# Four graph layers on one core: a first batch of its own, and 64-row products issued in blocks

## The chip, the core and the metric

The kernel runs on one core of one Trainium2 chip. The metric is device time in microseconds of that core, the median of several executions. Engines are named as in the profile: PE (TensorE; PEld its weight loads), DVE (VectorE), ACT (ScalarE), POOL (GpSimd), and SP (SyncE), which issues most DMAs.

## What is computed

There are 16 independent graphs ("batches") of N = 1024 nodes with D = 128 features, and a dense 1024 x 1024 matrix `adj` each, of which about 1.6% is nonzero. Four layers follow each other; each normalises `x`, applies relu, and adds its result to `x`. Cut to what matters:

```python
h = relu(layernorm(x))                       # before every layer
# layer 0: columns of adj, degree from its rows
x += relu(concat(h, (adj.T @ h) / adj.sum(-1)) @ W0.T + b0)
# layer 1: rows of adj
x += leaky(((adj / adj.sum(-1)) @ h) @ W1.T + b1)
# layer 2: two rounds l of edge scores; only nonzero adj[n, m] matter
s[n, m] = sigmoid(relu(a[n] + b[m] + be1[l]) @ We2[l] + be2[l])   # a, b: h @ We1[l]
msg = (adj * s) @ h ;  h = layernorm(h + mlp([h, msg]))
x += h
# layer 3: attention over the nonzeros, softmax by rows, elu
x += elu(softmax(masked(leaky((Wh1 + Wh2.T) * (adj + I)))) @ Wh)
```

## The kernel before

N is cut into T = 8 tiles of P = 128 nodes. Layer 2 is the large one. It handles the 36 unordered tile pairs (28 off the diagonal, 8 on it, `BUCKETS`) in nine groups of four (`GROUPS`), and keeps only nonzero edges, packed in slots (320 for a pair off the diagonal, 480 on it).

`first(b)` (line 1014) does layers 0 and 1 of a batch. It loads each row tile `at` and each column tile `ct` of `adj` (line 977), sums the rows and copies them (`deg`, line 1037), transposes them on PE (`tn`, 1040 and 1041), writes the transposed matrix to DRAM (`adjT`, 1043), marks the nonzero places (`has`, 1048) and multiplies column tiles by the features (`nb`, 545). `count` (1071) ranks the nonzeros, layer 1 reads `adjT` back as `l`, and `build` (1158) makes four 0/1 matrices per pair: `st` from `far` (1112, 1116), `onT` (1191), `omT` (1199) and `om` (1206), on PE, ACT and DVE in turn.

`main` and `round` run the two rounds of layer 2. `gather` (1334) makes the hidden values of a pair's edges: four products into one PSUM bank `pre` (1345 and 1351), then two `hid` operations on ACT and DVE (1366, 1367). `dots` (1375) turns them into scores with 24 or more one-column products. `scores` (1417) spreads them (`val`, 1443), and `scatter` (1451) places them back with products into the bank `p` (1488). For the second direction of a pair off the diagonal these products write only 64 of 128 partitions: six per pair, 24 per group. Seven of the nine groups have them, so there are 224 such sets in 16 batches and two rounds. `upd` (1495) and `messages` (1501) follow. `last(s, b)` (1573) is the end of layer 2 and layer 3 of a batch (`strip`, `e`, `hp`).

The order on each engine is not that of the program. `run` (1599) weaves the generators of batch b's `main`, batch b-1's `last` and batch b+1's `first`. Then the class `Issue` (66 to 297) takes all instructions of this part, gives each a cost (`costs`, 130), and walks through them with a ready list per engine (`walk`, 196), forward and backward for four passes; the plan with the earliest end becomes a fixed order of issue on every engine. A change between full and 64-row products costs 94 or 119 ns in that walk (`switched`, 192). Nothing is reordered at run time.

In `run`, batch 0 has a part of its own ahead of the loop: `first(0)` runs alone up to the start of its builds, with the small preparations in `scaled` (893) beside it. Its builds are then woven into batch 0's `main`.

A second program for inputs that do not fit the packed form (class `Pairs`) is built too, and does not run here.

Of the kernel before, what the change touches and what calls it, by code (L numbers as in the profile page):

```python
# [3 lines left out]

# [53 lines left out]

SIGNAL_NS = 45.0
RESULT_NS = {"PE": 163.0, "Activation": 120.0, "DVE": 88.0, "Pool": 80.0}  # L60
NARROW_NS, WIDE_NS, HELD_NS = 94.0, 119.0, 130.0
DMA_NS, DMA_NS_PER_BYTE, DMA_NS_BEHIND, DMAS = 1900.0, 3.9e-3, 3.3e-3, 8
PASSES = 4


class Issue:
# [3 lines left out]
    def __init__(self, tc, ops, fixed):  # L70
        self.tc, self.ops, self.fixed = tc, ops, fixed
        self.tiles = {t.name: t for t in tc.tiles}
        self.queue = [str(i.engine).split(".")[-1] for i in ops]
        self.kind = [type(i).__name__.removeprefix("Inst") for i in ops]
        self.links()
        self.costs()

    def span(self, arg):

# [50 lines left out]
    def costs(self):  # L130


        self.busy, self.late, self.form, self.bytes = [], [], [], []
        for op, queue, kind in zip(self.ops, self.queue, self.kind):
            out, form = op.outs[0].bass_ap, False
            n, late, size = self.size(op.outs[0]), RESULT_NS.get(queue, 0.0), 0
            aps = [a.bass_ap for a in op.ins if hasattr(a, "bass_ap")]
            psum = bool(aps) and aps[0].space == bass.MemoryType.PSUM
            if kind == "Matmult":
                n = self.size(op.ins[0])  # L140
                form = out.shape[0] < 128
                if op.ins[0].dtype == F32:
                    busy = max(n / 1.2 + 6, 112) * (1 if op.is_transpose else 2)
                else:
                    busy = 29 if form else max(n / 2.4 + 2.5, 25)
            elif kind == "DMACopy":
                size = n * WIDTH[op.outs[0].dtype] * out.shape[0]
                inside = all(a.space == bass.MemoryType.SB for a in (out, aps[0]))
                busy = 630 if inside else 470
                late = DMA_NS + size * DMA_NS_PER_BYTE - busy  # L150
            elif queue == "Activation":
                busy = n / 1.2 + (50 if psum else 92) + 92 * (len(aps) - 1)
            elif queue == "DVE":
                wide = [a for a in aps if a.size() > 128]
                fast = kind == "TensorScalarPtr" and len(wide) == 1 and not psum
                if kind in ("BNStats", "TensorReduce"):
                    n = self.size(op.ins[0])
                busy = n * (0.53 if fast else 1.0625) + 55 + 64 * (len(aps) - len(wide))
                rows = {v[1] for v in map(self.span, (*op.ins[:1], *op.outs[:1])) if v}
                busy += HELD_NS * (len(rows) > 1)  # L160
            else:
                busy = 1560
            self.bytes.append(size)
            self.busy.append(busy)
            self.late.append(busy + late)
            self.form.append(form)

    def joined(self):

# [20 lines left out]
        return users, turn, homes  # L190

    def switched(self, j, was, back):
        one, two = (self.form[j], was) if back else (was, self.form[j])
        return 0.0 if one == two else NARROW_NS if two else WIDE_NS

    def walk(self, rank, seq, back=False):

# [8 lines left out]
        free, sent, was = dict.fromkeys(queues, 0.0), [(0.0, 0.0, 0)] * DMAS, False  # L206

        def offer(j):

# [20 lines left out]
        for _ in range(n):  # L230
            at, q = min(
                (free[q] if now[q] else max(free[q], soon[q][0][0]), q)
                for q in queues if now[q] or soon[q]
            )
            while soon[q] and soon[q][0][0] <= at:
                heappush(now[q], heappop(soon[q])[1:])
            j = heappop(now[q])[1]
            more = 0.0
            if self.kind[j] == "DMACopy" and not back:
                at = max(at, sent[0][1])  # L240
                more = DMA_NS_BEHIND * sum(
                    n * (end - at) / (end - then) for then, end, n in sent if end > at
                )
                sent = sent[1:] + [(at, at + self.late[j] + more, self.bytes[j])]
            elif q == "PE":
                at += self.switched(j, was, back)
                was = self.form[j]
            start[j], free[q] = at, at + self.busy[j]
            line[q].append(j)
            end = at + (self.busy[j] if back else self.late[j] + more + SIGNAL_NS)  # L250
            freed = {}
            for name in self.uses[j]:
                users[name] -= 1
                over[name] = max(over.get(name, 0.0), end)
                if name not in turn:
                    continue
                tag = self.tiles[name].tag
                if name not in live:
                    live[name] = heappop(homes[tag])
                    freed.setdefault(tag, []).append(given[tag] + 1)  # L260
                    given[tag] += 1
                if not users[name]:
                    heappush(homes[tag], over[name])
                    freed.setdefault(tag, []).append(given[tag])
            for tag, keys in freed.items():
                for key in dict.fromkeys(keys):
                    for k in parked.pop((tag, key), ()):
                        offer(k)
            for k, lag in edges[j]:
                ready[k] = max(ready[k], at + lag + more * (lag > 0.0))  # L270
                waits[k] -= 1
                if not waits[k]:
                    offer(k)
# [27 lines left out]
def tile_four_gnn_layers(  # L301
# [22 lines left out]
    nc = tc.nc  # L324
    B, N, D = x.shape
    P = 128
# [117 lines left out]
    class Layers:  # L444
# [20 lines left out]
            return tile.rearrange("p (t d) -> p t d", d=P + 1)  # L465

        def small(self, shape, tag, name):
            return self.work.tile(shape, F32, tag=f"{tag}{self.lane}", name=name)

        def one(self, name):  # L470

# [327 lines left out]
    class Edges:  # L799
# [115 lines left out]
        def scale_terms(self):  # L915
# [15 lines left out]
            for l in range(L):  # L931
                for h in range(2):
# [4 lines left out]
            bnd = work.tile([P, L], F32, tag="end", name="bnd")  # L937
# [48 lines left out]
        def strip(self, name):  # L986

            if self.rows_of.get("c"):
                return flat(self.row("c", name))
            return self.work.tile([P, 2 * 3 * P], F32, tag="strip", name=name, bufs=1)  # L990

        def alone(self, lane, others):

# [20 lines left out]
        def first(self, b):  # L1014
# [2 lines left out]
            xt = self.work.tile([P, T, D], F32, tag="x", name=f"x_{b}")  # L1017
            nc.sync.dma_start(xt, x[b].rearrange("(t p) d -> p t d", p=P))
            for _ in lane.layer0_own(xt, name):
                if b:  # L1020
                    yield 1.3
            z, own = lane.z, lane.o
            yield 0

# [43 lines left out]
            s.x = self.kept(xt, "x", f"xk_{b}")  # L1068
            yield from self.build(s, has, name)

        def count(self, s, has, name):


# [11 lines left out]
            end = self.work.tile([P, nb], F32, tag="end", name=f"end_{name}")  # L1085
# [204 lines left out]
        class Group:  # L1290
# [43 lines left out]
            def gather(self, i):  # L1334
# [5 lines left out]
                for d in range(self.nd):  # L1340
                    pre = path.m.one(f"pre_{self.name}_{i}_{d}")

                    parts, _ = path.parts[u // Q]
                    for k in range(2):
                        nc.tensor.matmul(  # L1345
                            pre[:, :c], parts[:, k, u % Q, 1 - d], om,
                            start=(k == 0), stop=True, skip_group_check=True,
                        )
                    _, both = path.parts[t // Q]
                    for k, (at, first) in enumerate(((0, 0), (c - n, back))):  # L1350
                        ins = nc.tensor.matmul(  # L1351
                            pre[:, at : at + n], both[:, k, t % Q, d], st[:, first : first + n],
                            start=False, stop=True, skip_group_check=True,
                        )
                    if not self.diag:
                        hid = path.work.tile(
# [184 lines left out]

        def main(self, s, b):

            xT = self.back(self.m.scratch(f"xT_{b}"), s.xT)
            self.parts = [None] * NH
            for h, half in enumerate(self.halves_of(xT)):
                yield from self.split(self.m, 0, h, half, f"{b}")
# [269 lines left out]
```

## Time and profile before

| what | value |
|---|---|
| time, median of 3 runs | 4661.11 us (4647.63 to 4667.04) |
| the profiled execution | 4639.45 us, its span 4637.7 us, granted clock 0.982 |
| PE, DVE, ACT busy | 94%, 84%, 65% of the span |
| DMA | 603.41 MB, mean 130 GB/s |
| first `pre` of batch 0 | 124.6 us after the start of the span |
| from there to the first `pre` of batch 1 | 250.9 us |
| from a batch's first `pre` to the next one's, batches 1 to 14 | 278.8 to 285.0 us |
| from batch 15's first `pre` (4321.1 us) to the end | 316.6 us |

A busy share is a mean over stages with different limits, so the stages are looked at one by one below. In the profile a row such as `L1488 PE MATMUL p<-omT,val 128*64 128x128 fp8e4` names line, engine, operation, what is written and read, the columns of the array that are used (64 of 128) and the moving operand. Matmuls overlap, so their mean durations are longer than the time from the start of one to the start of the next.

### The profile page before, as it was taken

What the parts mean: (1) busy time and instruction counts of PE and PEld (TensorE: products, weight loads), DVE (VectorE), ACT (ScalarE), POOL (GpSimd) and SP (SyncE); (2) the same over time, 40 slices, a digit from 0 to 9 for tenths busy, and PEclk for the clock granted to TensorE, in tenths of its full rate; (3) what the DMA queues carried; (4) which work ended last, traced back from release to release, by engine and by line L of the source; (5) the groups of instructions that cost most, each with busy time, mean ns of one, the idle gap of its engine ahead of it and who ended that gap; (6) DMA issues with size and microseconds to landing.
All of it is one profiled execution on the core that took longest, in us unless ns stands there. A gap on an engine that the chain in (4) does not pass through costs nothing.

```text
span 4637.7 us, 132212 instructions
## 1 busy us (share of the span) xinstructions
PE 4359.0 (94%) x53685; PEld 3581.9 (77%) x53685; DVE 3873.0 (84%) x9128; ACT 2992.3 (65%) x7238; POOL 194.4 (4%) x137
## 2 busy tenths in 40 slices
PE   6999999999999999999999999999999999999986
PEld 5787778777787777878878787777877777788765
DVE  4777797987979889797897979879797897979977
ACT  5666575675756767576675766757576675766643
POOL 0000100000000000000000000000000000000000
PEclk7999999999999999999999999999999999999997
DMA  7262635445363542635436353453634436344221
GB/s 213 66 198 68 196 94 164 114 127 162 90 185 100 147 142 83 196 107 147 126 94 198 89 162 115 130 165 85 189 103 140 142 83 196 107 145 123 80 80 57
DMA packets 852857, 603.41 MB, mean 130 GB/s; under 512 B 128528, under 2 KB 782608, under 8 KB 852240
## 3 DMA queue, kind: packets, MB, share of 16 engines
q1 hardware_dynamic: 847136, 593.24, 44.3%
q8 instruction: 423, 6.93, 0.6%
q10 hardware_dynamic: 5104, 1.65, 0.1%
q14 instruction: 194, 1.59, 0.1%
HBM read 446.44 MB, written 100.66 MB: 118 GB/s over the span
## 4 chain that ended last, share of the span: by engine, by line
PE 63%; DVE 21%; ACT 6%; DMA 6%; issue 2%; SPq 1%; POOL 1%; ACTq 0%; DVEq 0%; POOLq 0%
PE pre L1345 8%; PE nb L545 8%; PE p L1488 7%; PE msg L441 7%; PE sc L1391 5%; PE pre L1351 5%; DVE hid L1367 4%; PE h L599 4%; DVE val L1443 3%; PE hp L441 3%; PE bb L553 2%; PE xn L608 2%; PE tn L1040 2%; DMA at<-in_adj_dram 2%; DMA both<-part 2%
## 5 line engine op out<-in xcount | busy, mean ns | idle before, releaser
L1367 DVE SCALAR_TENSOR_TENSOR hid<-pre,hid 128x320 f16<-128x320 f32 (+1 forms) x2048 | 1004.1, 508 | 168.6 <-ACT hid L1366 157.9
L1366 ACT ACTIVATE hid<-pre 128x320 f16<-128x320 f32 (+1 forms) x2048 | 906.0, 461 | 330.0 <-PE pre L1351 301.4
L1345 PE MATMUL pre<-om,part 128*128 128x320 fp8e4 (+1 forms) x4096 | 970.9, 309 | 9.8 <-DVE hid L1367 3.7
L1351 PE MATMUL pre<-st,both 128*128 128x176 fp8e4 (+1 forms) x4096 | 681.5, 244 | 21.9 <-DMA both<-part 21.5
L1443 DVE TENSOR_TENSOR val<-onT,u 128x1024 f32<-128x1024 fp8e4 x576 | 695.5, 1218 | 1.6
L441 PE MATMUL msg<-upd,xf 128*128 128x128 f32 (+3 forms) x3008 | 638.7, 327 | 3.8 <-DVE upd L1495 3.8
L1351 PEld LDWEIGHTS <-both 128*128 128x128 f16 x4096 | 392.6, 98 | 180.1 <-issue 35.9
L1391 PE MATMUL sc<-slide,hid 128*128 128x1 f16 x12800 | 435.4, 163 | 28.5 <-DVE hid L1367 26.4
L1391 PEld LDWEIGHTS <-hid 128*128 128x128 f16 x12800 | 410.0, 96 | 53.4 <-DVE hid L1367 40.9
L441 PEld LDWEIGHTS msg<-upd,xf 128*128 128x128 f32 x3008 | 414.4, 191 | 27.6 <-DVE upd L1495 5.5
L1412 ACT ACTIVATE tan<-sc,be_s,down 128x8 f32<-128x8 f32 (+1 forms) x960 | 296.6, 358 | 193.8 <-PE sc L1391 189.1
L1495 DVE SCALAR_TENSOR_TENSOR upd<-p,adj 128x512 f32<-128x512 f32 x512 | 351.6, 687 | 72.4 <-PE p L1488 70.5
L1206 ACT ACTIVATE om<-pm 128x320 fp8e4<-128x320 f32 (+1 forms) x576 | 270.4, 469 | 206.7 <-PE pm L1152 200.0
L1488 PE MATMUL p<-val,omT 128*128 128x64 f16 (+1 forms) x6528 | 373.0, 204 | 27.9 <-DVE val L1443 26.9
L1345 PEld LDWEIGHTS <-part 128*128 128x128 f16 x4096 | 345.2, 98 | 69.0 <-issue 36.8
L1488 PEld LDWEIGHTS <-omT 128*128 128x128 fp8e4 x6528 | 329.3, 97 | 55.0 <-issue 45.4
L441 PE MATMUL hp<-wh,e 128*128 128x129 f32 x2048 | 328.7, 287 | 16.7 <-DVE e L773 16.6
L1191 ACT ACTIVATE onT<-pn 128x256 fp8e4<-128x256 f32 (+1 forms) x576 | 252.3, 438 | 68.1 <-PE pn L1137 62.5
L441 PEld LDWEIGHTS hp<-wh,e 128*128 128x128 f32 x2048 | 274.3, 195 | 26.8 <-DVE e L773 21.7
L1116 DVE TENSOR_SCALAR st<-far,wid 128x384 fp8e4<-128x384 f16 (+1 forms) x576 | 238.6, 428 | 59.4 <-PE pre L1351 37.8
L1112 ACT ACTIVATE far<-iota_off,mid 128x384 f16<-128x384 f16 x448 | 270.0, 625 | 17.3 <-DVE st L1116 14.7
L545 PEld LDWEIGHTS nb<-z,l 128*128 128x128 f32 x2048 | 254.8, 194 | 33.8 <-issue 19.3
(224 smaller groups left out, 7890.8 us busy)
## 6 DMA issues: line engine op xcount, KB each, us to landing
at<-in_adj_dram SPq DMA_DIRECT2D x128, 512.0 KB, 5.1
ct<-in_adj_dram SPq DMA_DIRECT2D x128, 512.0 KB, 5.4
adjT<-tn SPq DMA_DIRECT2D x128, 512.0 KB, 6.3
l<-adjT SPq DMA_DIRECT2D x128, 512.0 KB, 5.8
adj<-adjT SPq DMA_DIRECT2D x256, 256.0 KB, 3.5
a<-adjT SPq DMA_DIRECT2D x128, 384.0 KB, 3.8
both<-part SPq DMA_DIRECT2D x256, 128.0 KB, 3.4
adj<-adjT SPq DMA_DIRECT2D x448, 64.0 KB, 2.6
```

The lines of the kernel that those rows point to most:

```text
L441: nc.tensor.matmul(dst, left, right, start=opened is None, stop=True, skip_group_check=True)
L545: nc.tensor.matmul(ps, mat[:, k], z[:, k], start=(k == 0), stop=(k == T - 1))
L1206: nc.scalar.activation(om, pm, AF.Copy, saturate=False)
L1345: nc.tensor.matmul(pre[:, :c], parts[:, k, u % Q, 1 - d], om, start=(k == 0), stop=True, skip_group_check=True,)
L1351: ins = nc.tensor.matmul(pre[:, at : at + n], both[:, k, t % Q, d], st[:, first : first + n], start=False, stop=True, skip_group_check=True,)
L1366: nc.scalar.activation(hid[:, 0, :c], pre[:, :c], AF.Relu)
L1367: nc.vector.scalar_tensor_tensor(hid[:, 1, :c], pre[:, :c], 0.0, hid[:, 0, :c], op0=OP.max, op1=OP.subtract)
L1391: nc.tensor.matmul(sc[:, k, g : g + 1], self.hid[self.done + g][:, v, at : at + P], sign, start=(g, v, k) == (*order[0], 0), stop=True, sk ...
L1412: nc.scalar.activation(dst, src, AF.Tanh, bias=path.be2[:, self.l : self.l + 1], scale=path.down[:, self.l : self.l + 1],)
L1443: nc.vector.tensor_tensor(val, onT[:, i : i + each].rearrange("p i (c n) -> p i c n", n=n), v.rearrange("p k i o -> p i k o").to_broadcast ...
L1488: nc.tensor.matmul(dst, left, right, start=n < first, stop=True, skip_group_check=True)
L1495: nc.vector.scalar_tensor_tensor(upd, ps, S_SCALE, self.adj[:, d * Q : (d + 1) * Q], op0=OP.add, op1=OP.mult,)
```

## The change

Six things change; the diff follows.

1. **A first batch of its own** (`opening` in place of `first(0)`). Its eight row tiles stay in SBUF, five in row buffers and three in buffers that layer 2 uses later. No column tile is loaded: for each row tile k the eight products with `z[:, k]` are added into two PSUM banks, and `has` is made from a row tile and an earlier transposed tile. The transposed tiles stay in SBUF too, and layer 1 reads them there. `adjT` is still written.
2. **All builds of batch 0 ahead of its `main`**, woven into its layer 1, in banks of their own (`a`, `p` and three of `pre`, while layer 1 has `c`, `acc0` and `acc1`). `main` of batch 0 takes `xT` from SBUF.
3. **Blocks** (`blocks`, and the pick in `walk`). Neighbouring 64-row products on the same bank form a block. Its first one gets the waits of all, and once PE is in a block, the walk stays in it.
4. **Another cost of a change of form** (`switched`): f32 products are a third form, and after a product shorter than 108 ns they cost the difference.
5. **The order in `gather`**: `part`, `both`, `both`, `part` in place of `part`, `part`, `both`, `both`.
6. **Buffers**: `strip` two instead of one; `bn`, `seen` and `end` one instead of two.

```diff
-                form = out.shape[0] < 128
+                form = "narrow" if out.shape[0] < 128 else "full"
                 if op.ins[0].dtype == F32:
+                    form = "wide"
...
+    def blocks(self):
+        line = [j for j in range(len(self.ops)) if self.queue[j] == "PE"]
+        self.block, run = {}, []
+        for j in (*line, None):
+            if j is not None and self.form[j] == "narrow" and (
+                not run or self.uses[j][-1] == self.uses[run[0]][-1]
+            ):
+                run.append(j)
+                continue
+            for k in run:
+                self.block[k] = run[0]
+                if k > run[0]:
+                    for i, done in self.needs[k].items():
+                        if i not in run:
+                            self.needs[run[0]][i] = self.needs[run[0]].get(i, False) or done
+            run = [j] if j is not None and self.form[j] == "narrow" else []
...
     def switched(self, j, was, back):
-        one, two = (self.form[j], was) if back else (was, self.form[j])
-        return 0.0 if one == two else NARROW_NS if two else WIDE_NS
+        if was is None:
+            return 0.0
+        k, i = (j, was) if back else (was, j)
+        one, two = self.form[k], self.form[i]
+        if one == two:
+            return 0.0
+        cost = NARROW_NS * (two == "narrow") + WIDE_NS * (one == "narrow")
+        return cost + max(0.0, LOAD_NS - self.busy[k]) * (two == "wide")
...
-            j = heappop(now[q])[1]
+            if q == "PE" and len(now[q]) > 1 and was in self.block:
+                best = min(now[q], key=lambda v: (self.block.get(v[1]) != self.block[was], v))
+                now[q].remove(best)
+                heapify(now[q])
+                j = best[1]
+            else:
+                j = heappop(now[q])[1]
...
-            return self.work.tile([P, 2 * 3 * P], F32, tag="strip", name=name, bufs=1)
+            return self.work.tile([P, 2 * 3 * P], F32, tag="strip", name=name, bufs=2)
...
+        def opening(self):
...
+            rows = [self.row("a", f"at_0_{t}") for t in range(5)]
+            rows += [
+                self.work.tile([P, T, P], F32, tag=tag, name=f"at_0_{5 + i}", bufs=1)
+                for i, tag in enumerate(("part0", "both0", "part1"))
+            ]
+            for t, at in enumerate(rows):
+                nc.sync.dma_start(
+                    at, adj[0, t * P : (t + 1) * P, :].rearrange("p (k n) -> p k n", n=P)
+                )
+            load_rest()
...
+            for k, at in enumerate(rows):
+                turned.append(lane.scratch(f"tn_0_{k}"))
+                nc.scalar.activation(turned[k], at, AF.Copy, accum_out=deg[:, 0, k : k + 1])
+                for ks, ps in lane.halves(f"tn_0_{k}"):
+                    for i, m in enumerate(ks):
+                        nc.tensor.transpose(ps[:, i], at[:, m], ident)
+                    nc.scalar.activation(turned[k][:, ks[0] : ks[-1] + 1], ps, AF.Copy)
+                nc.sync.dma_start(self.columns(s.adjT, k), turned[k])
+                for t in range(T):
+                    h = t // Q
+                    dst = sums[h][:, (t - h * Q) * P : (t - h * Q + 1) * P]
+                    opened[h] = add_to(opened[h], dst, at[:, t], z[:, k])
+                for t in range(k + 1):
+                    nc.vector.tensor_tensor(
+                        has[:, INDEX[t, k]], at[:, t], turned[t][:, k],
+                        op=OP.logical_or, saturate=False,
+                    )
+                if k == 4:
+                    self.scaled()
...
+            ours, theirs = [("c", 1), ("acc0", 1), ("acc1", 1)], [("a", 1), ("p", 1), ("pre", 3)]
+            for _ in lane.layer1(xt, lambda t: turned[t], deg[:, 1], name):
+                lane.banks = theirs
+                for us in s.builds:
+                    if us == 0.5:
+                        break
+                lane.banks = ours
...
-                    for k in range(2):
-                        nc.tensor.matmul(
-                            pre[:, :c], parts[:, k, u % Q, 1 - d], om,
-                            start=(k == 0), stop=True, skip_group_check=True,
-                        )
                     _, both = path.parts[t // Q]
-                    for k, (at, first) in enumerate(((0, 0), (c - n, back))):
-                        ins = nc.tensor.matmul(
-                            pre[:, at : at + n], both[:, k, t % Q, d], st[:, first : first + n],
-                            start=False, stop=True, skip_group_check=True,
+                    terms = [
+                        (pre[:, at : at + n], both[:, k, t % Q, d], st[:, first : first + n])
+                        for k, (at, first) in enumerate(((0, 0), (c - n, back)))
+                    ]
+                    ends = [(pre[:, :c], parts[:, k, u % Q, 1 - d], om) for k in range(2)]
+                    for k, (dst, left, right) in enumerate((ends[0], *terms, ends[1])):
+                        nc.tensor.matmul(
+                            dst, left, right, start=k == 0, stop=True, skip_group_check=True
                         )
...
-            xT = self.back(self.m.scratch(f"xT_{b}"), s.xT)
+            xT = self.back(self.m.scratch(f"xT_{b}"), s.xT) if b else s.xT0
...
-            first = self.first(0)
-            next(first)
-            load_rest()
-            for n, us in enumerate(first):
-                if us is None:
-                    break
-                if n == 8:
-                    self.scaled()
-
+            self.opening()
             self.alone(self.a, "")
             self.a.banks = [self.own["c"], self.own["a"]]
-            self.next.builds = first
```

More of the change, by code (lines that the diff above doesn't have):

```diff
@@ L1 @@
 from contextlib import ExitStack
-from heapq import heappop, heappush
+from heapq import heapify, heappop, heappush
 from itertools import chain, islice
@@ L60 @@
 RESULT_NS = {"PE": 163.0, "Activation": 120.0, "DVE": 88.0, "Pool": 80.0}
-NARROW_NS, WIDE_NS, HELD_NS = 94.0, 119.0, 130.0
+NARROW_NS, WIDE_NS, LOAD_NS, HELD_NS = 94.0, 119.0, 108.0, 130.0
 DMA_NS, DMA_NS_PER_BYTE, DMA_NS_BEHIND, DMAS = 1900.0, 3.9e-3, 3.3e-3, 8
 PASSES = 4
+STAY = 0.0
 class Issue:
@@ L76, in __init__ @@
         self.costs()
+        self.blocks()
     def span(self, arg):
@@ L140, in costs @@
                 n = self.size(op.ins[0])
-                form = out.shape[0] < 128
+                form = "narrow" if out.shape[0] < 128 else "full"
                 if op.ins[0].dtype == F32:
+                    form = "wide"
                     busy = max(n / 1.2 + 6, 112) * (1 if op.is_transpose else 2)
                 else:
-                    busy = 29 if form else max(n / 2.4 + 2.5, 25)
+                    busy = 29 if form == "narrow" else max(n / 2.4 + 2.5, 25)
             elif kind == "DMACopy":
@@ L205, in walk @@
         soon, now = {q: [] for q in queues}, {q: [] for q in queues}
-        free, sent, was = dict.fromkeys(queues, 0.0), [(0.0, 0.0, 0)] * DMAS, False
+        free, sent, was = dict.fromkeys(queues, 0.0), [(0.0, 0.0, 0)] * DMAS, None
         def offer(j):
@@ L246, in walk @@
                 at += self.switched(j, was, back)
-                was = self.form[j]
+                was = j
             start[j], free[q] = at, at + self.busy[j]
@@ L467, in small @@
         def small(self, shape, tag, name):
-            return self.work.tile(shape, F32, tag=f"{tag}{self.lane}", name=name)
+            more = {"bufs": 1} if tag in ("bn", "seen") else {}
+            return self.work.tile(shape, F32, tag=f"{tag}{self.lane}", name=name, **more)
         def one(self, name):
@@ L936, in scale_terms @@
                     )
-            bnd = work.tile([P, L], F32, tag="end", name="bnd")
+            bnd = work.tile([P, L], F32, tag="end", name="bnd", bufs=1)
             nc.vector.tensor_reduce(
@@ L1019, in first @@
             for _ in lane.layer0_own(xt, name):
-                if b:
-                    yield 1.3
+                yield 1.3
             z, own = lane.z, lane.o
@@ L1069, in first @@
             yield from self.build(s, has, name)
+        def opening(self):
+            s = self.next = Batch()
+            lane, name = self.a, "0"
+            xt = self.work.tile([P, T, D], F32, tag="x", name="x_0")
+            nc.sync.dma_start(xt, x[0].rearrange("(t p) d -> p t d", p=P))
+            rows = [self.row("a", f"at_0_{t}") for t in range(5)]
[8 more added lines that the diff above has]
+            load_rest()
+            for _ in lane.layer0_own(xt, name):
+                pass
+            z, own = lane.z, lane.o
+            s.adjT = self.dram.tile([N, N], F32, tag="adjT", name="adjT_0", bufs=3)
+            has = self.work.tile([P, len(BUCKETS), P], FP8, tag="has", name="has_0", bufs=1)
+            deg = self.work.tile([P, 2, T], F32, tag="deg", name="deg_0")
+            sums = [self.acc(h, f"nb0_0_{h}") for h in range(NH)]
+            opened, turned = [None] * NH, []
+            for k, at in enumerate(rows):
[17 more added lines that the diff above has]
+                    self.scaled()
+            nc.vector.reciprocal(deg[:, 1], deg[:, 0])
+            for t in range(T):
+                nc.vector.scalar_tensor_tensor(
+                    own[:, t], sums[t // Q][:, t % Q * P : (t % Q + 1) * P], deg[:, 1, t : t + 1],
+                    own[:, t], op0=OP.mult, op1=OP.add,
+                )
+            lane.layer0_end(xt, own)
+            self.count(s, has, name)
+            s.builds = self.build(s, has, name)
+            next(s.builds)
+            ours, theirs = [("c", 1), ("acc0", 1), ("acc1", 1)], [("a", 1), ("p", 1), ("pre", 3)]
[5 more added lines that the diff above has]
+                lane.banks = ours
+            s.xf = self.work.tile([P, T, D], F32, tag="xf0", name="xf0_0", bufs=1)
+            lane.normal(xt, s.xf, AF.Relu, f"2_{name}")
+            s.xT0 = lane.transposed(s.xf, f"2_{name}")
+            s.xT = self.kept(s.xT0, "xT", "xT0_0")
+            s.x = self.kept(xt, "x", "xk_0")
@@ L1084, in count @@
             s.wid = self.work.tile([P, nb], F32, tag="wid", name=f"wid_{name}")
-            end = self.work.tile([P, nb], F32, tag="end", name=f"end_{name}")
+            end = self.work.tile([P, nb], F32, tag="end", name=f"end_{name}", bufs=1)
             nc.vector.tensor_scalar(s.wid, s.cnt, -1.0, None, op0=OP.add)
@@ L1343, in gather @@
                     parts, _ = path.parts[u // Q]
-                    for k in range(2):
-                        nc.tensor.matmul(
-                            pre[:, :c], parts[:, k, u % Q, 1 - d], om,
-                            start=(k == 0), stop=True, skip_group_check=True,
-                        )
-                    _, both = path.parts[t // Q]
-                    for k, (at, first) in enumerate(((0, 0), (c - n, back))):
-                        ins = nc.tensor.matmul(
-                            pre[:, at : at + n], both[:, k, t % Q, d], st[:, first : first + n],
-                            start=False, stop=True, skip_group_check=True,
+                    _, both = path.parts[t // Q]
+                    terms = [
[4 more added lines that the diff above has]
+                    for k, (dst, left, right) in enumerate((ends[0], *terms, ends[1])):
+                        nc.tensor.matmul(
+                            dst, left, right, start=k == 0, stop=True, skip_group_check=True
                         )
```

## The prediction

> **What bounds the kernel now.** I read the page first: busy time, then the slices.
>
> ```profile
> PE 4359.0 (94%) x53685; PEld 3581.9 (77%) x53685; DVE 3873.0 (84%) x9128; ACT 2992.3 (65%) x7238; POOL 194.4 (4%) x137
> ...
> PE   6999999999999999999999999999999999999986
> ...
> DVE  4777797987979889797897979879797897979977
> ```
>
> PE looks like the bound of everything after the first slice. But VectorE's digits swing between 7 and 9, which a single bound does not explain. So I cut one batch (the sixth) in two: from its first `pre` of edge layer 0 (1508.2 us) to the first `pre` of group 1 of edge layer 1 (1678.0), and on to the next batch's first `pre` (1788.6). The windows view, with columns PE, PEld, DVE, ACT, POOL, granted clock, DMA share, GB/s:
>
> ```profile
> 1508.20:1678.00 169.80, 166.40 (x1892) 135.19 (x1890) 131.35 (x331) 107.06 (x250) 9.33 (x6) 0.99 0.55 158
> 1678.00:1788.60 110.60, 103.69 (x1460) 87.23 (x1457) 108.33 (x239) 79.12 (x202) 2.64 (x2) 0.98 0.33 96
> ```
>
> Part A is PE's (166.4 of 169.8 us). Part B is VectorE's (108.3 of 110.6, where the last batch's attention layer runs beside the edges). The next batch reads 163.7 of 168.4 and 110.3 of 113.9. A PE saving counts in A only.
>
> Then PE's timeline, in a stretch where the 64-row products are broken up:
>
> ```profile
> 1353.67 0.32 PE L515 MATMUL tp<-ident,h 128*128 128x128 f32 x1
> 1353.92 0.36 PE L1488 MATMUL p<-omT,val 128*64 128x128 fp8e4 x6
> 1354.21 0.33 PE L515 MATMUL tp<-ident,h 128*128 128x128 f32 x1
> 1354.47 0.25 PE L1488 MATMUL p<-omT,val 128*64 128x128 fp8e4 x2
> 1354.65 0.33 PE L515 MATMUL tp<-ident,h 128*128 128x128 f32 x1
> 1354.91 0.25 PE L1488 MATMUL p<-omT,val 128*64 128x128 fp8e4 x2
> ```
>
> A `tp` takes 109 ns from start to start among its like; here 0.26 us pass before the next `p`, and two `p` products (29 ns each in a long run) take 0.18.
>
> Last the opening, in the chain that ended last (start, us, what):
>
> ```profile
> 45.07 15.45 DMA at<-in_adj_dram x2
> 60.57 1.97 PE tn L1040 x8
> 62.54 2.44 PE nb L545 x16
> ...
> 69.17 2.51 ACT far L1112 x4
> ```
>
> and in three windows (columns as above):
>
> ```profile
> 75.00:79.00 4.00, 4.00 (x18) 3.71 (x18) 1.26 (x3) 2.83 (x6) 0.00 (x0) 0.50 0.00 0
> 87.00:95.00 8.00, 7.56 (x72) 7.38 (x71) 6.92 (x20) 7.72 (x14) 0.00 (x0) 1.00 0.97 274
> 110.00:118.00 8.00, 4.92 (x40) 3.80 (x40) 2.08 (x3) 4.77 (x11) 0.00 (x0) 0.50 0.37 113
> ```
>
> Until 62 us the loads of rows and columns set the pace; the first `pre` comes at 124.6. By then 8 of 36 pairs have their `onT`; the other 28 are built during batch 0.
>
> **The blocks of 64-row products (all 16 batches).** I took start-to-start times of PE's records. After a 176-column `pre` product the next full-width product starts 76 ns later, a 64-row one 169: 93 ns to go in. Leaving takes 152 where the product needs 29: 123 more. In the order of the built programs the 5376 products stand in 521 runs before and in 224 after, each of 24. That is 297 fewer visits x 216 ns = 64.2 us of PE time, 4.0 a batch.
>
> [...]
>
> **The gather's order of products.** An f32 product behind a short one waits for its weights: after 76 ns of `pre` its second pass comes after 145 ns instead of 111, after 136 ns of `pre` with no delay. So 108 ns minus the length of what precedes is lost. Before, 748 f32 products follow a 76-ns `pre`; after, 36 do, and 711 follow a 136-ns one. Over all kinds the sum falls from 88.2 to 65.7 us: 22.5 us of PE, 1.4 a batch.
>
> **What of these 86.7 us shortens a batch.** I costed each engine's instructions, in the order in which each program issues them, by these intervals (PE) and by VectorE's start-to-start times.
>
> Part A, PE: before 162.6 and 160.9 us in turn (measured 169.8 and 168.4, so 7.4 of waits); after 160.9 in every batch. Switches and weights give 3.3 less, but 2.5 us of other products move in from B.
>
> Part B: PE falls from 98.5 and 100.7 to 95.0, but VectorE has 111.0 and 111.1 before and 110.8 after. Measured are 110.0 (PE at 98.5) and 114.0 (PE at 100.7). After I take 110, as the lighter sort.
>
> So 160.9 + 7.4 + 110 = 278.3 us for batches 4 to 13, where 281.6 was measured: 10 x 3.3 = 33. The same sums for batches 2, 3 and 14 give 1.6 + 6.3 + 2.5. Sum: 43.4 us. The last batch and the tail keep their sums (PE 120.0 and 120.2 in its part A): nothing.
>
> **The opening.** Out go eight column loads and eight reads of `adjT` (8.4 MB), and the read-back of `xT`; 36 `has` operations of 0.29 us replace fifteen wider ones. Rows, x and first weights (4.9 MB) at the 238 GB/s of the page's queue in 20 to 40 us need 21 us and land by 26. Then others are late. ScalarE from its first `h` (12.35): 3.2 + 1.0 + 1.2 for `h`, `hT`, `z`, 8 x 1.16 for the row sums, 16 x 0.5 for `tn`, 1.6 of small ones, and about half of 9 us of DMA issues on its queue: 41. PE has 28 us of products from 12.9; at a granted clock of 0.83 as in 20 to 60 us it ends at 46. So the last `tn` is ready at 46 instead of 63.2.
>
> From there to the first `pre` the changed order has all 36 builds, layer 1 and the next batch's first steps. ScalarE carries most: 36 `far` 18.9, `om` 13.1, `onT` 11.8, `rank` 5.3, three normalisations 9.2, copies 9.6 = 68 us. VectorE has 51, PE 44. Ahead of it stand about 3.5 us: eight `own` updates now come together at the end. Fed at 96% as in 87 to 95 us, the first `pre` comes at 46 + 3.5 + 70.5 = 120, 4.6 us earlier. Bounds: always fed 117.5; fed as in 110 to 118 (60%) 163. I take the near end, since five PSUM banks serve the builds there and two did in 110 to 118.
>
> [...]
>
> What is gained is the work that batch 0 no longer does. Its PE work falls from 233.2 to 218.8. By parts: A 128.0 + its measured 12 of waits, B VectorE's 95.4 + 3 (half of its measured 5.7 of waits) = 238.4, measured 250.9: 12.5 less. Batch 1: 155.8 + 9.5 + 110.3 = 275.6 against 285.0: 9.4 less. Opening in all: 4.6 + 12.5 + 9.4 = 26.5.
>
> **What I cost at nothing.** Second `strip` buffer: in part B no instruction waits for the strips `a`, so an earlier load gains nothing. Single buffers for `bn`, `seen`, `end`: VectorE itself writes and reads them, in its own order, so no wait on another engine arises, save for `bnd`, once in the opening. The direct use of `xT` in batch 0 saves a read, and the wait for the write ahead of it, that hide under the last `far` and `om` of the opening (3 us, if they did not). SP: eight `adjT` writes stand before the first `adj` and next-batch loads; nobody needs these for 60 us. The block's wait: all 24 products of a block read one `val` operation (1.22 us) and one bank, ready together, so nothing is held back for a later one.
>
> **Sum.** 43.4 + 26.5 = 70. The profiled execution took 4639.45 us (span 4637.7), 0.5% under the median of 4661.11; the difference goes on the median: 4661 - 70 = 4591.
>
> **The rivals.** (1) As above: 4591, chance 0.62. (2) PE bounds everything, so 64.2 + 22.5 are kept, and the opening's PE waits fall from 124.6 - 55 to 120 - 75, by 24.6: 111 less, 4550. For it: PE's 94%. Against: part B's row. 0.17. (3) The other way: a merged order only moves waits in A too, and the 26.5 of the opening remain: 4635. For it: A's sum falls by under 1 us. 0.13. (4) Slower: VectorE starves behind the block. A visit was 10.3 products on average, 0.51 us; a block is 24 x 29 + 216 = 0.91. In B VectorE has three `pre` banks, about 1.5 us of `hid`; a block next to a run of 24 score products (0.6) uses that up. If each of B's 7 blocks costs VectorE 0.9 us, 15 batches lose 95 and it ends at 4686; it decides from 70 / 105 = 0.67 us a block. Against: VectorE also holds `val`, `upd` and attention work between. 0.08. That the blocks aren't formed is excluded by the order.
>
> **Numbers.** A measurement of this kernel tells about 0.5% (23 us) from no change. Cases 1 and 2 (0.79) are faster beyond that, and two thirds of case 3 (0.08), which ends 3 us past the line; the rest of case 3 (0.05) and 0.03 of case 4 fall within it; 0.05 of case 4 are slower. Faster 0.87, same 0.08, slower 0.05. The range reaches from case 2 to past case 3: 4540 to 4650.
>
> **What would show it.** Right: 224 visits; part A near 168, part B near 110 with VectorE at 98% and PE near 95 of work; first `pre` at 115 to 130 with all 36 `onT` done; batch 0 near 238. Wrong: part B under 107 (then case 2), first `pre` past 135 with a clock of 0.50, or VectorE idle before `hid` behind the blocks (case 4).

## The result and the profile after

The changed kernel took 4599.34 us (median of 4 runs, 4593.86 to 4604.73), the kernel before 4660.0 beside it: a ratio of 0.9873, 95% interval [0.9848, 0.9897]. The forecast was 4591, so 8 us more than foreseen. That near hit is in part luck: terms missed in both directions.

Busy times and two rows of slices from the page:

```profile
PE 4329.6 (94%) x53685; PEld 3587.1 (78%) x53685; DVE 3856.4 (84%) x9142; ACT 3005.5 (65%) x7238; POOL 191.4 (4%) x137
...
PE   7999999999999999999999999999999999999986
...
DVE  6787896988969889698897979879798896988886
```

The shares are the same as before, although the kernel is shorter; in PE's row only the first slice changed. As before, the answer lies in the stages. The sixth batch again, part A (to the first `pre` of group 1 of edge layer 1) and part B (to the next batch); columns PE, PEld, DVE, ACT, POOL, granted clock, DMA share, GB/s:

```profile
1474.90:1644.20 169.30, 165.44 (x1894) 135.07 (x1893) 131.58 (x330) 108.34 (x254) 9.23 (x6) 1.00 0.54 156
1644.20:1756.40 112.20, 103.52 (x1467) 87.83 (x1465) 108.24 (x239) 79.30 (x199) 2.69 (x2) 0.95 0.34 101
```

A is still full of PE and B of VectorE. Look at the clock in B: 0.95, where it was 0.98. (PE's busy time counts a product at half clock as longer work: an f32 pass took 213 ns at 0.50 and 109 to 112 at 1.00.) Over batches 4 to 13, A averages 169.0 us (169.6 before) and B 111.2 (112.0).

The blocks do what was computed. PE's timeline in the changed kernel:

```profile
1506.36 0.74 PE L1493 MATMUL sc<-slide,hid 128*128 128x1 f16 x24
1507.04 0.86 PE L1590 MATMUL p<-omT,val 128*64 128x128 fp8e4 x24
1507.83 0.29 PE L1240 MATMUL pn<-eye,st 128*128 128x64 f16 x3
```

All 24 products stand together, and 0.79 us pass from the first to the next operation; 24 x 29 ns and 123 ns for leaving were 0.82. The weights' waits went too: 711 f32 products follow a 136-ns `pre`, and their second pass comes after 109 ns (median), where it came after 145 behind the 76-ns ones of before.

The opening has another chain. It ran through loads of `at` before; now, from the write of a transposed tile at 31 us on (start, us, what):

```profile
31.41 6.61 DMA adjT<-tn
38.08 0.37 SPq L1139
38.54 0.53 SPq L1423
39.12 5.76 DMA a<-adjT
44.91 0.49 DVE a L802 x2
45.63 1.90 DVE own L1153 x7
48.20 1.13 DVE x L611
...
55.41 3.08 ACT h L543 x8
```

and in two windows from 49 us, where the last `tn` is ready, to the first `pre` at 114.1:

```profile
49.00:79.00 30.00, 26.63 (x286) 24.28 (x287) 20.47 (x63) 28.86 (x69) 1.64 (x1) 0.89 0.26 68
79.00:114.10 35.10, 30.35 (x308) 25.96 (x308) 27.09 (x76) 33.44 (x81) 3.27 (x2) 0.85 0.21 55
```

ScalarE (the fourth pair of numbers) is busy for 62.3 of 65.1 us, 96%: it carries the builds.

Stage by stage, from the two profiled executions (spans 4637.7 and 4595.7). The column "again" is a second profile of the kernel before (e0, span 4652.2):

| stage | before | again | after | change from before | forecast |
|---|---|---|---|---|---|
| to the first `pre` | 124.6 | 119.6 | 114.1 | -10.5 | -4.6 |
| batch 0 | 250.9 | 253.2 | 241.9 | -9.0 | -12.5 |
| batch 1 | 285.0 | 285.7 | 275.1 | -9.9 | -9.4 |
| batches 2, 3, 14 | 844.8 | 845.9 | 847.3 | +2.5 | -10.4 |
| batches 4 to 13 | 2815.8 | 2826.2 | 2801.9 | -13.9 | -33 |
| batch 15 and the tail | 316.6 | 321.5 | 315.3 | -1.3 | 0 |

The sum is 42, not 70. The medians differ by 61, mostly because the profiled execution of before (4639.45) lies below the timed runs beside it; against the second profile the sum is 56. So one profile places batches 4 to 13 to about 1 us a batch (281.6 and 282.6): the gain there is 1.4 to 2.4 a batch where 3.3 were forecast. It places the opening no better: the first `pre` came at 119.6 to 124.6 in three profiles with the old opening (e2 the third) and at 114.1 to 117.7 in eleven with the new one. The means, 121.8 and 116.1, differ by 5.7 and not by 10.5.

One row of the waits is new. Before, then after (us in total, times, longest):

```profile
PE tp L1536 <- DVE xf L627: 1.7, 7, 0.5
```

```profile
PE tp L1638 <- DVE xf L663: 43.7, 15, 3.2
```

This is the hand-over from the first edge round to the second, at the start of part B: PE transposes the half of `xf` that VectorE has just normalised. In the old order PE had other work there. In the new one it stands still for about 3 us in every batch from batch 2 on. PE in the sixth batch, before and after:

```profile
1684.91 0.96 PE L1536 MATMUL tp<-ident,xf 128*128 128x128 f32 x4 [0.19 <-DVE xf L627]
```

```profile
1651.64 1.11 PE L1638 MATMUL tp<-ident,xf 128*128 128x128 f32 x4 [3.07 <-DVE xf L663]
```

and the windows around it in the changed kernel:

```profile
1644.20:1648.20 4.00, 2.83 (x49) 2.25 (x47) 4.00 (x14) 1.90 (x6) 1.01 (x1) 1.00 0.49 165
1648.20:1652.20 4.00, 0.93 (x7) 0.66 (x6) 4.00 (x15) 0.85 (x2) 0.00 (x1) 0.77 0.26 103
1652.20:1656.20 4.00, 3.85 (x37) 3.11 (x36) 2.64 (x9) 0.70 (x2) 0.00 (x0) 0.50 0.17 66
1656.20:1660.20 4.00, 4.00 (x43) 3.46 (x42) 3.53 (x9) 2.90 (x7) 1.68 (x1) 0.87 0.00 0
```

The second to last triple is the clock: 0.77, 0.50, 0.87. In half-microsecond windows it falls to 0.50 near 1650.4 and is back near 1657.2, so PE does the work from 1651.6 to 1657.2 at half speed and loses another 2.8 us (an estimate: half of 5.6). Length times (1 - clock), summed over the B parts of batches 4 to 13, is 18 us before (10 in the second profile) and 45 after. What this costs in time is not shown: VectorE (third pair) works all through PE's wait, and what it waits for PE's `bb` behind it rose only from 36.3 to 46.3 us in the whole run.

### The profile page after: what moved, and what is told of

It reads as the page before. It is cut to its first block, busy times and chain, and to the rows that moved or that the text cites. A ratio compares the mean times of both kernels' runs of the same rounds, so it can differ in the third digit from the quotient of the medians.

```text
span 4595.7 us, 132099 instructions
## 1 busy us (share of the span) xinstructions
PE 4329.6 (94%) x53685; PEld 3587.1 (78%) x53685; DVE 3856.4 (84%) x9142; ACT 3005.5 (65%) x7238; POOL 191.4 (4%) x137
## 4 chain that ended last, share of the span: by engine, by line
PE 47%; DVE 37%; ACT 6%; DMA 6%; issue 3%; POOL 1%; SPq 1%; DVEq 0%; ACTq 0%; POOLq 0%
PE pre L1454 10%; DVE hid L1469 8%; PE nb L581 7%; PE p L1590 5%; DVE val L1545 5%; PE h L635 4%; PE msg L476 4%; DVE upd L1597 3%; PE sc L1493 3%; DVE omT L1302 3%; DVE e L803 3%; PE bb L589 2%; PE tn L1075 2%; DVE e L807 2%; PE xn L644 2%
## 5 line engine op out<-in xcount | busy, mean ns | idle before, releaser
L1454 PE MATMUL pre<-om,part 128*128 128x320 fp8e4 (+1 forms) x4096 | 1160.4, 310 | 25.1 <-DVE hid L1469 13.0
L1468 ACT ACTIVATE hid<-pre 128x320 f16<-128x320 f32 (+1 forms) x2048 | 917.0, 462 | 357.2 <-PE pre L1454 340.7
L1469 DVE SCALAR_TENSOR_TENSOR hid<-pre,hid 128x320 f16<-128x320 f32 (+1 forms) x2048 | 1001.8, 508 | 107.4 <-ACT hid L1468 98.7
L476 PE MATMUL msg<-upd,xf 128*128 128x128 f32 (+3 forms) x3008 | 627.7, 323 | 7.8 <-DVE upd L1597 7.8
L476 PEld LDWEIGHTS msg<-upd,xf 128*128 128x128 f32 x3008 | 424.8, 191 | 24.5 <-DVE upd L1597 10.8
L1590 PE MATMUL p<-val,omT 128*128 128x64 f16 (+1 forms) x6528 | 400.3, 206 | 19.6 <-DVE val L1545 18.5
L1454 PEld LDWEIGHTS <-part 128*128 128x128 f16 x4096 | 392.7, 99 | 21.9 <-issue 7.8
L1590 PEld LDWEIGHTS <-omT 128*128 128x128 fp8e4 x6528 | 353.3, 98 | 55.3 <-issue 32.8
L1294 ACT ACTIVATE onT<-pn 128x256 fp8e4<-128x256 f32 (+1 forms) x576 | 254.4, 443 | 110.5 <-PE pn L1240 101.9
L635 PE MATMUL h<-xm,wu_sb 128*128 128x512 f32 x512 | 262.2, 605 | 10.3 <-DMA xm<-xTk 8.9
```

Source lines behind the costliest of these rows:

```text
L476: nc.tensor.matmul(dst, left, right, start=opened is None, stop=True, skip_group_check=True)
L635: nc.tensor.matmul(ps, wu1_sb[:, l, i, kb * P : (kb + 1) * P], src, start=(i == 0), stop=(i == 1),)
L1454: nc.tensor.matmul(dst, left, right, start=k == 0, stop=True, skip_group_check=True)
L1468: nc.scalar.activation(hid[:, 0, :c], pre[:, :c], AF.Relu)
L1469: nc.vector.scalar_tensor_tensor(hid[:, 1, :c], pre[:, :c], 0.0, hid[:, 0, :c], op0=OP.max, op1=OP.subtract)
L1590: nc.tensor.matmul(dst, left, right, start=n < first, stop=True, skip_group_check=True)
```

## The experiments

Three questions: what each part of the change is worth (e1 to e4), what bounds part B (e5, e6, e8, e9, e11), and how much is due to the order that the planner happens to find (e7, e10). Each kernel but e0 is the changed one with an edit. "Against the changed kernel" is the difference of the two ratios to the kernel before, times 4655 us; it carries about 14 us of uncertainty. The planner made a new order for e1 to e4, e7, e10 and e11; e5, e6 and e8 keep the order of the changed kernel, and e9 all of it but the products that it moves.

| run | median | ratio to before, interval | against the changed kernel |
|---|---|---|---|
| e0 | 4653.34 | 0.9991 [0.9978, 1.0005] | |
| e1 | 4638.03 | 0.9976 [0.9967, 0.9984] | +48 |
| e2 | 4614.49 | 0.9927 [0.9907, 0.9948] | +25 |
| e3 | 4671.48 | 1.0056 [1.0036, 1.0077] | +85 |
| e4 | 4617.17 | 0.9938 [0.9918, 0.9958] | +30 |
| e5 | 4577.27 | 0.9825 [0.9808, 0.9842] | -22 |
| e6 | 4597.43 | 0.9870 [0.9854, 0.9887] | -1 |
| e7 | 4550.73 | 0.9775 [0.9759, 0.9791] | -46 |
| e8 | 4551.45 | 0.9782 [0.9765, 0.9798] | -42 |
| e9 | 4627.9 | 0.9951 [0.9934, 0.9967] | +36 |
| e10 | 4526.41 | 0.9733 [0.9715, 0.9751] | -65 |
| e11 | 4516.56 | 0.9696 [0.9673, 0.9719] | -82 |

**e0, the kernel before once more**, for a second profile.

> The kernel before, once more, for a second profile: the first one's execution (4639 us) lies 0.45% under the median, so the two profiles differ by 42 us where the medians differ by 61. Expected: ratio 1.000 within 0.3%; a span near 4655 us if the first profile was a fortunate execution, with the extra spread over all batches.

It gave the column "again" above; 2826.2 us are 282.6 a batch.

**e1, the opening and the buffers alone**: no blocks, the old cost of a change of form, the old order in `gather`.

```diff
-        self.blocks()
+        self.block = {}
...
-        cost = NARROW_NS * (two == "narrow") + WIDE_NS * (one == "narrow")
-        return cost + max(0.0, LOAD_NS - self.busy[k]) * (two == "wide")
+        return 0.0 if one == two else NARROW_NS if two else WIDE_NS
```

> The opening and its buffers, with the planner's costs, the gather's order and the free interleaving of 64-row products as before (554 visits). Theory of two bounds (PE in part A of a batch, VectorE in part B): the opening and the first two batches keep the 29 us that the changed kernel's profile shows there, and the later batches have PE 160.2 + VectorE 113.7 = 273.9 us by this order against 272.8 before, 1 us each the other way: about 4645 us, 15 below before. Rival, PE bounds everything: PE's work is 4190 us against 4181, so 29 - 9 = 20 below before.

11 us faster than before. Batch 2 starts at 641.7, 17 us ahead of e0 (658.5), but batches 4 to 13 need 284.5 each, 1.9 more than in e0: part of the lead is given back.

**e2, the old opening**: all of the change but points 1 and 2.

```diff
-            self.opening()
+            first = self.first(0)
+            next(first)
+            load_rest()
```

> Blocks, new costs of a change of form and new gather order, with the opening of before. Two bounds: the order of batches 2 to 14 has the same sums as in the changed kernel (3528 us against 3529), so what is lost is the opening's part, 20 to 29 us: 4620 to 4628 us. If the opening's lead is given back later by a wait elsewhere, under 10 us are lost.

25 us slower. Batch 2 starts 26 us later than in the changed kernel (657.0 and 631.1), and batches 4 to 13 take 280.1 as there.

**e3, no blocks**, and **e4, the old order in `gather`**:

```diff
-        self.blocks()
+        self.block = {}
```

```diff
-                    for k, (dst, left, right) in enumerate((ends[0], *terms, ends[1])):
...
+                    for k in range(2):
...
+                            pre[:, :c], parts[:, k, u % Q, 1 - d], om,
```

> The changed kernel without blocks (the walk may break up the 64-row products: 374 visits instead of 224). PE's work rises by 37 us. Two bounds: by this order batches 1 to 14 have sums that are 38 us longer (part A shorter by 2, part B's VectorE work longer by 5 each): about 4637 us. PE alone: 37 longer, 4636. Rival, the blocks only move waits: no change from 4599.

> The changed kernel with the gather's products in the old order (part, part, both, both), so that f32 products follow a 76-ns product again: weight waits 82.8 us instead of 65.7. PE alone: 17 us longer, 4616. Two bounds: sums of batches 1 to 14 are 24 us longer (part B's VectorE work 114.6 instead of 110.8): about 4623. If the weight waits are hidden: no change.

e3 has 374 visits to the 64-row form, and by the prediction's intervals 37 us more PE work; it lost 85 us. It is even slower than e1, which has 554 visits. So its loss cannot be the price of the switches alone. Its order is another one: batches 4 to 13 average 168.4 in A and 117.2 in B, where VectorE's busy time is 113.4 against 108.0. e4 likewise: 165.8 and 115.7. Work has crossed from A to B, where VectorE has no room. A kernel planned afresh differs by more than its edit, so e3 and e4 don't price the blocks or the order in `gather`, and no run takes out the new cost of a change of form alone.

**e5, less VectorE work, and e6, less PE work, both with the order held**. e5 leaves out the mask of attention's `e` on 96 of 128 columns, e6 part of the sums in `gather` (the last product of the second round covers 32 columns). The planner is told the old sizes, so the order stays.

```diff
-                    nc.vector.scalar_tensor_tensor(e, at, 0.0, e, op0=OP.is_gt, op1=OP.mult)
+                    part = slice(0, 32)
+                    ins = nc.vector.scalar_tensor_tensor(
+                        e[:, :, part], at[:, :, part], 0.0, e[:, :, part], op0=OP.is_gt, op1=OP.mult
+                    )
+                    AS_IF[ins.ins.name] = 2 * n * P
```

```diff
+                        m = 32 if (k, self.l) == (3, 1) else right.shape[1]
+                        ins = nc.tensor.matmul(
+                            dst[:, :m], left, right[:, :m], start=k == 0, stop=True,
```

> The changed kernel in the same order on every engine, but the masking multiply of the attention layer covers 32 columns of each strip row instead of all (the rest of the mask is left out): 12 VectorE operations per batch fall from 0.69 to 0.96 us to about 0.15, 8.6 us per batch, nearly all in part B. Two bounds: part B falls by up to 8.6 us (to VectorE's 102 or until PE's 95 with its waits is late), 15 batches: 90 to 130 us less, about 4490. PE alone: no change, 4599 less 10 at most.

> The changed kernel in the same order on every engine, but in the second round of the edge layer the last of the four gather products covers 32 columns instead of all (part of the low halves is left out). PE's work falls by 91 us by the intervals, 5.1 us per batch in part B and 0.6 in part A. PE alone: about 91 us less, 4508. Two bounds: part B stays with VectorE; 0.6 us per batch and some of the last round's, 10 to 20 us less, about 4584.

By the prediction's intervals e6 takes out 91 us of PE work, and it gains nothing that can be measured: PE alone doesn't set part B. But neither does VectorE. Part B of the sixth batch in e5:

```profile
1643.30:1755.20 111.90, 103.62 (x1467) 88.32 (x1463) 104.47 (x239) 79.06 (x199) 2.69 (x2) 0.95 0.35 101
```

VectorE is busy for 104.5 instead of 108.2 us, and the part is 0.3 shorter (0.7 in the mean of batches 4 to 13). The rest is waits. What VectorE waits for in that part, in the changed kernel and in e5:

```profile
DVE bb L1327 <- PE bb L589: 1.8, 2, 1.4
DVE hid L1469 <- ACT hid L1468: 1.0, 1, 1.0
DVE a L802 <- DMA a<-adjT: 0.3, 1, 0.3
DVE e L809 <- ACT e L808: 0.2, 1, 0.2
```

```profile
DVE hid L1475 <- ACT hid L1474: 2.0, 4, 1.1
DVE bb L1333 <- PE bb L591: 1.8, 2, 1.3
DVE omT L1308 <- PE pq L1304: 1.1, 3, 0.7
DVE a L804 <- DMA a<-adjT: 0.6, 1, 0.6
DVE u L1533 <- ACT u L1532: 0.5, 1, 0.5
DVE e L812 <- ACT e L810: 0.2, 1, 0.2
```

3.3 us have become 6.2: VectorE, quicker now, waits longer for PE and ScalarE in the fixed order. The cut itself was smaller than expected: VectorE's busy time fell by 6.4 us a batch and not by 8.6, 3.8 of them in B (means of batches 4 to 13) and 2.5 in A. By the theory of two bounds 15 x 3.8 = 57 us should still have come out, not 22 (8 to 36 with its uncertainty). So it fell for part B, and a second was formed: both engines are near their limit there, and with a held order each waits for the other in turn ("interlocked").

**e8, both cuts together, order held.**

> The order of the changed kernel is held, and both cuts are made at once: VectorE's masking multiply covers 32 of its columns (the mask is left out on the rest), and TensorE's last gather product of the second round covers 32 columns (part of its sum is left out). Alone the first gave 22 us and the second 2 us less than the changed kernel. 'Interlocked' (in part B the two engines wait for one another in turn, so that relieving one moves the wait to the other): both together give clearly more than 24 us, 60 to 130 us less, 4470 to 4540. 'Something else' (ScalarE, or the latency from engine to engine, sets part B): the two add up, 4570 to 4580. 'VectorE bounds B' as in the prediction: no more than the first alone, 4577.

42 us less. That is clearly more than e5 alone (they differ by 0.0043, each interval about 0.0017 to either side), and less than the 60 to 130 expected. Against the sum of the two, 24, the excess is 18 us, and its uncertainty, worked out from the four intervals, is 18 as well. Part B:

```profile
1634.00:1744.60 110.60, 100.64 (x1465) 86.58 (x1462) 103.94 (x239) 78.37 (x199) 2.69 (x2) 0.94 0.34 102
```

The mean B of batches 4 to 13 is 111.2, 110.5 (e5), 111.3 (e6) and 109.5 (e8). This points to the interlock without proving it, and most of the freed time stays unused: with VectorE busy for 4.1 us less and PE for 3.2, 1.7 come out. The clock takes a part: the same length times (1 - clock), over the B parts of batches 0 to 14, is 71 us in the changed kernel, 85 in e6 and 83 in e8. What holds the remainder is open.

**e9, one following product moved into the middle of a block** wherever it was ready, in the order of the changed kernel: 405 visits instead of 224.

```diff
+                pe[at : at + size + 1] = [*pe[at : at + size // 2], x, *pe[at + size // 2 : at + size]]
```

> The order of the changed kernel, save that in each block where it can be done one following product is put into the block's middle: 405 visits instead of 224, 181 more, by the prediction's 93 + 123 ns and the weights' waits 42 us more of TensorE work, 1.2 us a batch in part A and 1.3 in part B. 'TensorE bounds everything': 42 us more than the changed kernel, 4641. 'Two bounds': only part A's share counts, 18 us more, 4617. 'Interlocked': A's share and some of B's, 4620 to 4640. 'Planner': what the blocks gave came from the order that the planner found with them and not from the switches saved, then within 10 us of the changed kernel, 4599 to 4609.

36 us for 181 visits, 0.20 us each, with the 14 us of uncertainty 0.12 to 0.28. This run measures the price by itself, as far as all of it shows in the time. With the intervals of the trace it would be 42 us, if all counts, and that fits. In batches 4 to 13 A is 1.2 longer in the mean (1.2 worked out), B 0.6 (1.3): all seems to count in A and half in B, though the two profiles of before differ by as much in A (169.6 and 170.9). That rules out "planner" (under 10) and, barely, "two bounds" (18). "TensorE bounds everything" (42) lies within the uncertainty here; e6 speaks against it.

**e7 and e10, more passes of the planner**, nothing else.

```diff
-PASSES = 4
+PASSES = 24
```

(12 in e7.)

> The changed kernel with 12 passes of the planner instead of 4, nothing else. PE's work and VectorE's are the same in sum (4095 and 3766 us). PE alone: no change. Two bounds: the order splits them better, the sums of batches 1 to 14 are 80 us shorter (part B's VectorE work 104 to 112 instead of 110.8, PE's part A 148 to 161): at most 80 less, 4520; where both engines are now nearly full in both parts, waits take some of that, and I expect half, about 4560.

> The changed kernel with 24 passes of the planner instead of 4 (12 gave 4551, 48 us less, with the same work on each engine). 'The order sets part B': by the same sums over the instructions in their order (larger of TensorE's and VectorE's in each part, batches 4 to 13) 272 us a batch with 4 passes, 267 with 12 and 261 with 24: another 20 to 60 us less, 4490 to 4530. 'The 12 passes were luck' : no better than with 12, 4545 to 4600.

The work on each engine is the same, and the time falls by 46 and 65 us: as much as the whole change gave. e10 beats both kernels. It does so in another way than expected. The sums over its order fell by 11 us a batch in batches 4 to 13; measured are 280.2 to 277.0, and most of the rest comes from batches 2, 3 and 14 (14.5, 9.4 and 12.4 us). Its sixth batch:

```profile
1440.30:1590.80 150.50, 147.33 (x1791) 121.34 (x1788) 128.88 (x293) 101.54 (x240) 5.57 (x4) 1.00 0.46 133
1590.80:1711.80 121.00, 116.53 (x1566) 98.16 (x1565) 111.08 (x277) 86.52 (x215) 6.56 (x4) 1.00 0.49 145
```

A hundred PE instructions have moved from A to B, PE is near full in both, and the clock is 1.00. The hand-over's wait is nearly gone, and length times (1 - clock) over the B parts of batches 4 to 13 falls from 45 to 19 us:

```profile
PE tp L1638 <- DVE xf L663: 6.1, 5, 3.1
```

In e7 batches of both kinds lie in one run: 8 to 13 have the wait of 3.1 us and take 280.7 in the mean, 2 to 7 and 14 have none over 0.2 and take 273.8, with nearly the same work in each. Batch 7 among these, without the wait, took 280.0. Their orders differ in more than that wait, so this is a sign and no proof.

**e11, e5's cut with the planner free to use it** (the mask left out on the same columns):

> VectorE's masking multiply on 32 of its columns (the mask is left out on the rest), and the planner may plan with the shorter time, where the run with the held order gave 22 us less than the changed kernel. 'Order' (a relief of VectorE pays only where the order is made for it): well below the held order's 4577, 4500 to 4555. 'Something else sets part B': 4565 to 4590.

82 us less where the held order gave 22. Part B has VectorE at 108.0 in the mean, filled up again, and is 0.8 shorter than in the changed kernel; A falls from 169.0 to 165.3, as PE's busy time there falls from 165.4 to 160.9. Room on VectorE in B went with less PE work in A. How much of the 82 is the cut's is open: a longer search without any cut gave 46 and 65.

## Why the forecast was near, point by point

- **Price of a visit and of a weight wait**: right. The blocks are 224, a block ends as computed, and e9 gives 0.20 us (0.12 to 0.28) for 0.216. The weights' price is read from the trace alone (109 ns for 145), since e4's order is another.
- **Part A is PE's**: right. A is 3.8 shorter in e11 where PE's busy time is 4.5 less. Its waits, kept at 7.4, were 169.0 - 160.9 = 8.1.
- **"After I take 110, as the lighter sort"**: the failed step of the steady batches. The sum had VectorE at 110.8, and 111.2 was measured; the discount below the sum had no ground. The two errors, 0.7 in A's waits and 1.2 in B, make 1.9 us a batch, 19 in ten: that is what batches 4 to 13 fell short by.
- **"Part B is VectorE's"**: right in size, wrong as a cause. VectorE is busy for 97% of B, but a cut of 3.8 us there (e5) gives 0.7, and the rest turns into waits for the other engines. "PE bounds everything" fell with e6.
- **"What I cost at nothing"** left out the hand-over between the rounds. It is PE's largest wait now: 43.7 us of standing, and the clock after it. The built order was the place to look for it: what PE has queued between the last `pre` it can do and the `tp` of `xf`. e1 to e4 all have it (37.4 to 41.8 us), with and without blocks and with both openings, so neither alone brings it. The buffers are common to all, and no run took them back; but e7 and e10 have the same buffers and lose a third of it and most of it (27.9 and 6.1 us) by a longer search, so the buffers alone don't force it. Which part brings it, and what it costs, stays open.
- **The opening**: right mechanism, sizes off in its favour. ScalarE carries it at 96%, but with 62.3 us of work after 49 us instead of 68 after 49.5: hence 114.1 instead of 120. The gain, though, was forecast from a single profile of before; over all profiles it is 5.7 us, near the 4.6. The second `strip` buffer was not free here: its early load `a` stands before the `own` updates on VectorE, which waits 2.3 us for it at 42.6 us. e2 gives 25 us for the opening, 26.5 were worked out.
- **Batches 2, 3 and 14**: 12.9 us short. Batch 2 takes 287.5, with PE's busy time in A at 168.6 (164.1 before), and batch 14 has the largest loss of clock of all B parts before the last, 9.0 us. The sums over the order saw neither.
- **The clock in the opening**: granted were 0.89 and 0.85, between the 0.50 and the 1.00 in the rows of before (75 to 79 us and 87 to 95). The forecast has PE's 44 us as they are and ScalarE last, and ScalarE stayed last. PE does not wait in the row of 75 to 79 (4.00 of 4.00 busy at 0.50): it had waited 6.4 us up to 72.1, and the clock came back only at 80.9.
- **Only the opening remains** (4635): no. Without the new opening e2 is still 0.9927, 34 us below the kernel before.
- **VectorE starves behind the blocks** (the slower rival): no. All idle time of VectorE ahead of its `hid` fell from 168.6 to 107.4 us.

## What to carry to other kernels

When two engines are both above 90% in a stage with a fixed order, the one with the higher number need not be the bound: here relieving it by 3.8 us gave 0.7 there. With a new order the gain can appear in another stage, and the cut is then hard to tell from the new order. Where a planner makes the order, vary its search alone first: here that moved the time by as much as the change did, so a single re-planned kernel does not measure its edit. And look at the hand-overs in the new order: here TensorE's wait of 3 us was followed by 5.6 us of work at half its clock.

## What was not expected of the hardware

The clock fell in the hand-over only 1.8 us after PE's last product, and stayed at 0.50 for 6.8 us, 5.6 of them with PE fed again. In the 3.4 us ahead of this fall PE was busy for 1.0 us. From 300 us on every change of the clock in the changed kernel lies on a grid of 3.41 us steps. In the steps ahead of all 29 falls PE was busy for 2.5 us or less; the least in a step at full clock without a fall, up to 100 us before the end, was 1.9 (from 4135.3 us). In e0, though, three falls of 30 come behind a step in which PE was busy throughout. Less work on PE went with a lower clock as well: the mean granted over the span is 0.976 in the changed kernel and 0.970 in e6 and e8.
